# A graph-attention kernel on one core: three of four masks on GpSimd, a pair loop in fixed issue order with longer distances between its stages, and gelus in place in PSUM

## The chip, the cores and the metric

The kernel runs on one core of a Trainium2 chip. The metric is device time in microseconds (us), as the median over several executions; smaller is better. All numbers of a kernel come from the same program, once timed in rounds that alternate with the kernel before on the same chip, and once with the profiler on. A ratio given below is the mean time of one kernel's fast runs over the mean of the other's fast runs of the same rounds, so it is not quite the ratio of the two medians that I quote.

## The reference

Two layers over 3327 nodes with 64 features. Cut to what matters, with `_layernorm`, `proj`, `expmap` and the like as in any hyperbolic graph network:

```python
# layer 0, for every pair (i, j) of nodes
adj_att = sigmoid(left[:, None] + right[None, :] + b_att[0]) * adj
x_local = logmap(x[:, None, :], x[None, :, :], c)      # per pair, 64 features
support_t = einsum('ij,ijd->id', adj_att, x_local)
x = x + proj(expmap(h, support_t, c), c)
# layer 1
mask = (adj != 0)
rank = cumsum(mask, axis=1); deg = rank[:, -1:]
k = minimum(deg, 100)
pos = rank - (deg - k)
w = mask * where(pos > 0, 0.5 ** (k - pos), 0.0)
x = x + w @ (relu(layernorm(x)) @ weight) + bias
```

The kernel pads the nodes to 3328, which is 26 blocks of 128. The part that costs time is everything that has one number per pair: 3328 x 3328 of them. `logmap` is turned into a factor per pair, a product of two gelus that approximates the function of the distance, times the half-sigmoid, times `adj`; the sum over j is then a matmul. The mask and its running count for layer 1 are made in the same pass over `adj`.

## The kernel before

Columns are worked in four strips of 8, 8, 6 and 4 blocks, that is 1024, 1024, 768 and 512 columns; the last strip takes two blocks of rows at a time, so a full round is 1024 (or 768) columns wide everywhere. There are 26 + 26 + 26 + 13 = 91 rounds. `V` is VectorE, `A` ScalarE, `T` TensorE, `G` GpSimd.

```python
steps = iter(())
for b0, nb in STRIPS:
    # ... load the strip's operands; left broadcast by nb transposes and a copy
    for hi in range(NB, 0, -per):
        lo = max(hi - per, 0)
        js = range(hi - 1, lo - 1, -1)
        ad = work.tile([P, FMAX], F32, name="ad", bufs=4)
        nc.sync.dma_start(ad[...], adj_t[...])
        mask = work.tile([P, FMAX], BF16, name="mask", bufs=3)
        V.tensor_scalar(mask[:, :span], ad[:, :span], 0.0, None, op0=ALU.not_equal)
        for j in js:                                    # the running count, in PSUM
            for f0, f1 in hv:
                if before is not None:
                    T.matmul(pc[:, f0:f1], ca, before[:, f0:f1], ...)
                T.matmul(pc[:, f0:f1], cb, now[:, f0:f1], ...)
            if j % (2 if b0 == 0 else 4):               # the count is read out
                A.activation(kept, pc[:, :F], AF.Relu)
            else:
                V.tensor_scalar(kept, pc[:, :F], 0.0, None, op0=ALU.max)
        sg = work.tile([P, FMAX], F32, name="sg", bufs=3)
        for j in js:                                    # half-sigmoids
            A.activation(part(sg, j), left_b[:, :F], AF.Tanh, bias=right[:, j : j + 1], scale=0.5)
        V.scalar_tensor_tensor(sg, sg, 1.0, ad, op0=ALU.add, op1=ALU.mult)      # "sg combine"
        pq = ps.tile([P, FMAX], F32, name="pq", bufs=2)
        for j in js:                                    # products of the pair, in PSUM
            T.matmul(part(pq, j, f0, f1), ju[:KB, j, :], iuf[:, f0:f1], ...)
            T.matmul(part(pq, j, f0, f1), jz[:, j, :], izf[:, f0:f1], ...)
        s = work.tile([P, FMAX], F32, name="s", bufs=3)
        A.activation(s, pq, AF.Gelu, scale=-WG / QS)
        A.activation(s, s, AF.Gelu, scale=WH)
        V.scalar_tensor_tensor(s, s, WD, sg, op0=ALU.add, op1=ALU.mult)         # "final combine"
        for j in js:                                    # sums over j
            T.matmul(po[: D + 1, f0:f1], hw[:, j, :], part(s, j, f0, f1), ...)
            next(steps, None)                           # one step of the strip before's per-node work
    for _ in steps:
        pass
    # ... copy po out, transpose it
    steps = post(agg[:, :nb], b0, nb)
```

`post` is the per-node work of a finished strip: 17 VectorE instructions of 512 columns and, between them, 65 tiny ones of 8 columns. It is a generator that yields between groups of instructions. In this kernel the framework's scheduler decides in which order the instructions of an engine are issued; the program text only gives it priorities.

## Time and profile before

The kernel before took 461.72 us as a median of 3 runs.

In profile lines PE is TensorE and PEld its weight loads, DVE is VectorE, ACT ScalarE and POOL GpSimd; L842 is line 842 of the kernel and x91 a count. SBUF and PSUM are the two memories in which the program's tiles lie: those of the pool `ps` (`pq`, `pc`, `po`) in PSUM, all others here in SBUF.

The first lines here are from the profile page of the kernel before: busy time of each engine with its share of the span. Then groups of instructions: line, engine, operation, operands, shape, count, then busy us and mean ns of one, then idle time of the engine just before them with what ended most of it.

```profile
PE 378.4 (82%) x1484; PEld 153.4 (33%) x1484; DVE 407.1 (89%) x774; ACT 369.2 (80%) x423; POOL 13.3 (3%) x30
...
L842 DVE SCALAR_TENSOR_TENSOR sg<-sg,ad 128x1024 f32<-128x1024 f32 (+1 forms) x91 | 103.5, 1141 | 7.5 <-ACT sg L841 7.3
L852 DVE SCALAR_TENSOR_TENSOR s<-s,sg 128x1024 f32<-128x1024 f32 (+1 forms) x91 | 104.8, 1152 | 3.7 <-ACT s L851 3.6
...
L847 PE MATMUL pq<-iu,ju 71*128 71x512 f16 (+1 forms) x182 | 67.8, 374 | 11.6 <-ACT s L850 11.6
...
L824 DVE TENSOR_SCALAR mask<-ad 128x1024 bf16<-128x1024 f32 (+1 forms) x91 | 59.3, 654 | 3.4 <-PE pc L829 1.8
```

The reader should see that VectorE is the fullest engine, that masks are a seventh of its work, and that TensorE's products hardly wait (11.6 us over the whole run).

### The profile page before, as it was taken

How to read it: one execution, taken by the hardware profiler on the slowest of the kernel's cores; microseconds unless marked ns; L12 is line 12 of the kernel's file. 1: busy time of each engine (PE TensorE's matmuls, PEld its weight loads, DVE VectorE, ACT ScalarE, POOL GpSimd, SP SyncE). 2: the span in 40 equal slices, each digit the busy share in tenths (PEclk: the TensorE clock that was granted, in tenths of full speed). 3: DMA queues.
4: the chain of work that ended last, by engine and by line, in shares of the span. 5: the costliest groups of instructions: out<-in, count | busy, mean ns of one | idle time of the engine just before them, and what ended most of it. 6: DMA issues, size and time to landing. Idle time of an engine off the chain costs nothing.

```text
span 459.1 us, 4660 instructions
## 1 busy us (share of the span) xinstructions
PE 378.4 (82%) x1484; PEld 153.4 (33%) x1484; DVE 407.1 (89%) x774; ACT 369.2 (80%) x423; POOL 13.3 (3%) x30
## 2 busy tenths in 40 slices
PE   0266699999989799999997999889778897699293
PEld 0035233333323233333333444434322332244152
DVE  3895689999988999999998999999999998999821
ACT  1445989999894999999995999999599995888310
POOL 6000000000000000001000000020000000000000
PEclk9997699999999999999999999999999998899877
DMA  7103354545541444444442444344533420000003
GB/s 201 62 1 72 105 168 143 141 151 163 167 135 46 133 143 140 137 137 137 137 127 75 136 137 140 106 128 125 168 93 111 121 89 1 1 1 1 0 0 82
DMA packets 22840, 47.77 MB, mean 104 GB/s; under 512 B 8652, under 2 KB 9082, under 8 KB 22808
## 3 DMA queue, kind: packets, MB, share of 16 engines
q1 hardware_dynamic: 20522, 46.47, 34.7%
q10 hardware_dynamic: 2062, 0.87, 0.9%
q0 software_dynamic: 224, 0.07, 0.3%
q8 instruction: 13, 0.21, 0.2%
q14 instruction: 19, 0.16, 0.1%
HBM read 45.22 MB, written 0.85 MB: 100 GB/s over the span
## 4 chain that ended last, share of the span: by engine, by line

## 5 line engine op out<-in xcount | busy, mean ns | idle before, releaser
L855 PE MATMUL po<-s,hw 128*65 128x512 f32 (+1 forms) x364 | 165.3, 576 | 11.5 <-DVE s L852 11.1
L842 DVE SCALAR_TENSOR_TENSOR sg<-sg,ad 128x1024 f32<-128x1024 f32 (+1 forms) x91 | 103.5, 1141 | 7.5 <-ACT sg L841 7.3
L852 DVE SCALAR_TENSOR_TENSOR s<-s,sg 128x1024 f32<-128x1024 f32 (+1 forms) x91 | 104.8, 1152 | 3.7 <-ACT s L851 3.6
L841 ACT ACTIVATE sg<-left_b,right 128x1024 f32<-128x1024 f32 (+2 forms) x104 | 102.7, 1001 | 0.1
L851 ACT ACTIVATE s<-s 128x1024 f32<-128x1024 f32 (+1 forms) x91 | 91.4, 1006 | 0.1
L850 ACT ACTIVATE s<-pq 128x1024 f32<-128x1024 f32 (+1 forms) x91 | 87.7, 969 | 2.6 <-PE pq L848 2.6
L829 PE MATMUL pc<-mask,ca 128*128 128x512 bf16 (+1 forms) x175 | 65.7, 375 | 17.3 <-DVE behind_hi L836 7.2
L855 PEld LDWEIGHTS po<-s,hw 128*65 128x65 f32 x364 | 45.2, 138 | 98.9 <-issue 52.7
L847 PE MATMUL pq<-iu,ju 71*128 71x512 f16 (+1 forms) x182 | 67.8, 374 | 11.6 <-ACT s L850 11.6
L830 PE MATMUL pc<-mask,cb 128*128 128x512 bf16 (+1 forms) x182 | 66.7, 376 | 5.3 <-DVE mask L824 5.1
L848 PE MATMUL pq<-iz,jz 128*128 128x512 f16 (+1 forms) x182 | 66.6, 371 | 0.0
L824 DVE TENSOR_SCALAR mask<-ad 128x1024 bf16<-128x1024 f32 (+1 forms) x91 | 59.3, 654 | 3.4 <-PE pc L829 1.8
L894 PE MATMUL pw<-wt,s 128*128 128x512 bf16 (+1 forms) x182 | 41.0, 390 | 12.9 <-DVE s L782 9.2
L834 ACT ACTIVATE behind_hi<-pc 128x1024 uint8<-128x1024 f32 (+2 forms) x37 | 31.8, 860 | 24.3 <-PE pc L830 24.1
L830 PEld LDWEIGHTS <-cb 128*128 128x128 bf16 x182 | 17.9, 99 | 57.8 <-issue 46.6
L834 ACT ACTIVATE behind_lo<-pc 128x1024 uint8<-128x1024 f32 (+2 forms) x33 | 28.2, 853 | 7.1 <-PE pc L830 6.4
L894 PEld LDWEIGHTS <-s 128*128 128x128 f16 x182 | 18.7, 103 | 35.0 <-DVE s L782 9.6
L848 PEld LDWEIGHTS <-jz 128*128 128x128 f16 x182 | 18.1, 99 | 31.5 <-issue 15.3
L829 PEld LDWEIGHTS <-ca 128*128 128x128 bf16 x175 | 17.5, 100 | 30.8 <-issue 19.5
L847 PEld LDWEIGHTS <-ju 71*128 71x128 f16 x182 | 18.1, 100 | 21.4 <-issue 4.8
L836 DVE TENSOR_SCALAR behind_lo<-pc 128x1024 uint8<-128x1024 f32 (+2 forms) x19 | 19.9, 1050 | 1.1 <-PE pc L830 1.1
L771 POOL TENSOR_TENSOR x_sb<-x_sb,bias_b 128x512 f32<-128x512 f32 (+2 forms) x4 | 6.3, 1577 | 418.4 <-DVE w L769 418.4
(209 smaller groups left out, 290.0 us busy)
## 6 DMA issues: line engine op xcount, KB each, us to landing
ad<-in_adj_t SPq DMA_DIRECT2D x65, 512.0 KB, 3.7
ad<-in_adj_t SPq DMA_DIRECT2D x26, 384.0 KB, 3.3
out<-o SPq DMA_DIRECT2D x6, 128.0 KB, 2.0
x_sb<-in_x SPq DMA_DIRECT2D x1, 416.0 KB
x_sb<-in_x ACTq DMA_DIRECT2D x1, 416.0 KB, 6.9
iz<-jz ACTq DMA_DIRECT2D x2, 128.0 KB
iz<-jz SPq DMA_DIRECT2D x2, 128.0 KB, 2.4
iz<-jz SPq DMA_DIRECT2D x2, 96.0 KB
```

Source lines behind the costliest of these rows:

```text
L829: T.matmul(pc[:, f0:f1], ca, before[:, f0:f1], start=False, stop=True, skip_group_check=True)
L830: T.matmul(pc[:, f0:f1], cb, now[:, f0:f1], start=False, stop=True, skip_group_check=True)
L834: A.activation(kept, pc[:, :F], AF.Relu)
L841: A.activation(part(sg, j), left_b[:, :F], AF.Tanh, bias=right[:, j : j + 1], scale=0.5)
L842: V.scalar_tensor_tensor(sg[:, :span], sg[:, :span], 1.0, ad[:, :span], op0=ALU.add, op1=ALU.mult)
L847: T.matmul(part(pq, j, f0, f1), ju[:KB, j, :], iuf[:, f0:f1], start=True, stop=False)
L848: T.matmul(part(pq, j, f0, f1), jz[:, j, :], izf[:, f0:f1], start=False, stop=True)
L850: A.activation(s[:, :span], pq[:, :span], AF.Gelu, scale=-WG / QS)
L851: A.activation(s[:, :span], s[:, :span], AF.Gelu, scale=WH)
L852: V.scalar_tensor_tensor(s[:, :span], s[:, :span], WD, sg[:, :span], op0=ALU.add, op1=ALU.mult)
L855: T.matmul(po[: D + 1, f0:f1], hw[:, j, :], part(s, j, f0, f1), start=j == NB - 1, stop=j == 0)
L894: T.matmul(pw[n], s2[:, j].rearrange("p c d -> p (c d)"), wt[:, f0:f1].bitcast(BF16), start=j == 0, stop=j == NB - 1)
```

## The change

The intent: VectorE is full, so most masks go to GpSimd, which was idle; gelus are written back over their PSUM input, so that the final combine has only one SBUF operand; and the loop is written as a software pipeline with a fixed issue order on three engines, with loads five rounds ahead, masks four, counts three, sums two rounds behind, and no gap between strips. To make room on ScalarE, more of the count reads go to VectorE. The core of the diff, with cuts:

```diff
+AHEAD = 3
+SGB, ADB = 5, 7
+ON_ACT = ((1, 3), (1, 2), (1, 2), (1, 2))
...
+    def edges(n):
+        mask_of[n] = mask = work.tile([P, FMAX], BF16, name="mask", bufs=3)
+        args = mask[:, : span(n)], ad_of[n][:, : span(n)]
+        if n % 4 == 3:
+            V.tensor_scalar(*args, 0.0, None, op0=ALU.not_equal)
+        else:
+            G.tensor_scalar(*args, 0.0, 0.0, op0=ALU.is_equal, op1=ALU.is_equal)
...
-                if j % (2 if b0 == 0 else 4):
+        num, den = ON_ACT[k]
+        if (NB - 1 - j) % den >= den - num:
             A.activation(kept, ..., AF.Relu)
         else:
             V.tensor_scalar(kept, ..., 0.0, None, op0=ALU.max)
...
+    with tc.manual_schedule(engines={DVE, Activation, PE}):
+        products(0)
+        sigmoids(0)
+        for n in range(R):
+            m, w = n + AHEAD, span(n)
+            ...                                   # load(m + 2)
+            if turned: pa = turn(k - 1)           # transposes of the strip before
+            elif n > 1: total(n - 2)              # sums two rounds behind
+            A.activation(pq, pq, AF.Gelu, scale=-WG / QS)
+            A.activation(pq, pq, AF.Gelu, scale=WH)
+            if turned: steps = per_node(k - 1, pa)
+            V.scalar_tensor_tensor(sg, sg, 1.0, ad, op0=ALU.add, op1=ALU.mult)
+            edges(m + 1)
+            ...                                   # count(m), read(m), sigmoids(n + 1)
+            products(n + 1)
+            for _ in js(n):
+                next(steps, None)                 # a per-node step, whole, here
+            if lo == 0:
+                for _ in steps: pass
+            if ended: strip_out(k - 1)
+            V.scalar_tensor_tensor(sg, pq, WD, sg, op0=ALU.add, op1=ALU.mult)
```

Beside this the broadcast of `left` comes by DMA in strips 1 to 3 in place of transposes and a copy, a range check moves from the first change of strip to the end, and the matmul that gave each strip's count its start value is gone.

## The prediction

> **What bounds the kernel now.** I read the page's busy shares first (DVE 89%, PE 82%, ACT 80%, POOL 3%): three engines are nearly full, so an average can't name the bound. The second view is the time between two second gelus (the ScalarE line 851 in the timeline), one per round: it gives the four strips and the changes between them. The rounds run from 49 to 383 us; the gaps of 11.65, 10.86 and 11.43 us between neighbours (138.3, 242.4 and 324.6 us) are the changes of strip. The third view is the busy time of each engine in those stretches:
>
> ```profile
> core 0: us, PE busy (x) PEld busy (x) DVE busy (x) ACT busy (x) POOL busy (x), PEclk, DMA share, GB/s
> 49.00:139.00 90.00, 85.80 (x278) 30.60 (x278) 83.20 (x84) 85.06 (x89) 0.00 (x0) 0.96 0.52 154
> 150.00:242.00 92.00, 85.99 (x285) 29.89 (x283) 90.94 (x154) 91.25 (x99) 2.19 (x1) 1.00 0.48 138
> 253.00:325.00 72.00, 64.83 (x279) 29.32 (x278) 71.60 (x154) 71.15 (x98) 2.40 (x1) 1.00 0.47 134
> 336.00:383.00 47.00, 40.03 (x128) 13.23 (x126) 45.88 (x99) 45.87 (x68) 1.00 (x1) 1.00 0.35 101
> ...
> 242.00:253.00 11.00, 8.30 (x41) 3.88 (x42) 8.95 (x14) 5.78 (x9) 0.00 (x0) 1.00 0.21 67
> 325.00:336.00 11.00, 9.33 (x43) 4.00 (x42) 9.98 (x17) 5.48 (x10) 0.00 (x0) 1.00 0.35 107
> ```
>
> The reader sees: in strip 0 (first row) no vector engine is full, in strips 1 to 3 VectorE and ScalarE are both at 98 to 99%, and at a change of strip ScalarE falls to half while VectorE keeps 82 to 91%. DMA is at half.
>
> Durations overlap (the next instruction starts before the last has ended), so I take the cost of one from start to start in the timeline:
>
> ```profile
> 191.17 0.69 DVE L824 TENSOR_SCALAR mask<-ad 128x1024 bf16<-128x1024 f32 x1
> ...
> 191.77 0.69 DVE L752 TENSOR_TENSOR u<-u,w 128x512 f32<-128x512 f32 x1
> ...
> 192.37 0.38 PE L829 MATMUL pc<-mask,ca 128*128 128x512 bf16 x1
> ...
> 192.37 1.22 DVE L852 SCALAR_TENSOR_TENSOR s<-s,sg 128x1024 f32<-128x1024 f32 x1
> 192.59 0.38 PE L830 MATMUL pc<-mask,cb 128*128 128x512 bf16 x1
> ...
> 193.51 1.22 DVE L842 SCALAR_TENSOR_TENSOR sg<-sg,ad 128x1024 f32<-128x1024 f32 x1
> ```
>
> A mask costs VectorE 0.60 us (191.17 to 191.77), a combine 1.14 (192.37 to 193.51; I use 1.13, the median), a half matmul PE 0.216. Read in the same way: a count read out of PSUM 1.13 on VectorE and 0.90 on ScalarE; tanh 1.04, first gelu 0.90, second gelu 0.95 on ScalarE; the four fp32 passes of a sum 1.72 on PE (190.22 to 191.94). A PE round is 8 x 0.216 + 1.72 = 3.45 us; strip 0 ran at 90.2/26 = 3.47. So strip 0 is bound by PE, and strips 1 to 3 (rounds of 3.70, 2.86 and 3.93 us) by VectorE, with ScalarE just behind.
>
> **What the Trainium skill says.** (1) "SBUF — State Buffer", section "Who interferes with whom": GpSimd shares a port pair with VectorE; a VectorE instruction in a 2-port mode, or with two SBUF inputs against a GpSimd one that reads SBUF, excludes it for the whole instruction, and whoever comes second blocks; one SBUF input does not contend. The trace agrees. The 384-wide add on GpSimd, alone beside a PSUM read, took 1.00 us, the 256-wide one 0.73, so 512 should take 1.0 + 0.27 = 1.27; it took 2.19 behind a combine, and then a mask that takes 0.69 took 1.18 behind it:
>
> ```profile
> 215.38 1.22 DVE L852 SCALAR_TENSOR_TENSOR s<-s,sg 128x1024 f32<-128x1024 f32 x1
> 215.55 2.19 POOL L771 TENSOR_TENSOR x_sb<-x_sb,bias_b 128x512 f32<-128x512 f32 x1 [207.49 <-DVE w L769]
> 216.51 0.68 DVE L773 TENSOR_REDUCE t<-dt 128x8 f32<-128x512 f32 x1
> 217.11 1.18 DVE L824 TENSOR_SCALAR mask<-ad 128x1024 bf16<-128x1024 f32 x1
> ```
>
> (2) "GPSIMD Engine Reference", section "Engine selection": one-input work is roughly at line rate, two-input work about twice as slow; its clock is 1.2 GHz. A mask of 1024 columns is then, as an estimate from that page, 1024/1.2 = 0.85 us, and with about 0.2 of start (1.00 - 384 x 0.27/128 = 0.19 in this trace) some 1.1 us. No one-input instruction of this width is in the trace; a compare with two operations may be twice that. (3) "VectorE: DVE Perf Modes", section "Why PSUM operands drop a tier": an fp32 operand in PSUM runs at one element a cycle. The combine is already there, and a PSUM read costs the same 1.13 here as an SBUF combine, so moving its input to PSUM costs VectorE nothing. (4) "ScalarE: Activation LUTs", section "Step-by-step: what each stage is for": PSUM is the faster destination for ScalarE. Here a PSUM source gives 0.90 against 0.95 us.
>
> **The change, part by part.**
>
> Masks: of 91 rounds 3 in 4 leave VectorE: -0.75 x 0.60 = -0.45 us per 1024-wide round, -0.35 at 768 columns. Count reads move the other way: VectorE does 18 instead of 13 in strip 0 and 13 instead of 7 in the others. Strip 0: +5/26 x 1.13 = +0.22; strip 1: +6/26 x 1.13 = +0.26; strip 2: +6/26 x 0.87 = +0.20; strip 3, two reads of 512 per round: +2 x 6/26 x 0.60 = +0.28. Net on VectorE: -0.23, -0.19, -0.15, -0.17 per round. In strips 1 to 3, which it bounds: 26 x 0.19 + 26 x 0.15 + 13 x 0.17 = 11 us. Strip 0 gains nothing: PE's matmuls stay.
>
> ScalarE: second gelu out of PSUM, -0.05; fewer reads, -0.21 in strip 1: 3.40 instead of 3.66. It drops out of the race, which is needed but gains nothing itself.
>
> The combine with the gelus in place has one SBUF input, so it can't collide with a GpSimd mask; the other combine and the per-node steps can.
>
> Changes of strip: fixed order, counts three ahead, sums two behind, the broadcast of left by DMA instead of eight transposes and a copy. From 150 to 390 us VectorE's own idle time is 240 less about 232 busy, so at most 8 us come back there; I take 6. Strip 0 and its end last from 49 to 150, 101 us; PE needs 26 x 3.45 = 90 and about 4 more for the cold clock (matmuls of 0.43 until 57 us). I take 5 of the 7.
>
> Outside the rounds: range work leaves the start (about 1 us), its end moves under the decoding, left goes to memory and back: 0.
>
> GpSimd collisions: 49 masks in strips 1 to 3. A mask may start when the count two rounds later is through, which is close to the end of a VectorE round, where the contending combine starts. If one in three costs half a mask, 49 x 0.33 x 0.55 = 9 us come back.
>
> Fixed order stalls: the two-round loop final combine, products (0.86), two gelus (1.8), combine (1.13) is about 4.6 us with hops, against two rounds of 7: no stall. But an order can't fill a late wait with other work; I put -5 us of the gain on that.
>
> Sum: 461.7 - 11 - 6 - 5 + 9 + 5 = 453.7 with all the losses, 439.7 with none. I do not expect both losses in full: about 443.
>
> **The rivals.** (A) The port lock gives all back: if a mask takes 2 us and always meets a combine, each of 49 costs about 0.5, 25 us, and the time is near 461. For it: the 1.18 us mask above. Against: PSUM reads and the PSUM combine, 1.7 us of each round, are safe ground for it. (B) The fixed order is worth more than I credit: if VectorE, at 99% busy, hid waits that were only moved, the bound is PE, 84.5 full rounds x 3.45 = 292 against 341 now; with ramp and VectorE's per-node work it gives about 428. Against: VectorE's remaining work in the loop, combines 192, reads 54, per-node steps 45, masks 13, copies 4, is about 308, more than PE's, and all of the per-node part falls in strips 1 to 3. (C) GpSimd becomes the bound: it needs masks over 4/3 x 3.5 = 4.7 us; then rounds stretch and the time passes 465. I hold it unlikely, as a 512-wide two-input add takes 1.27.
>
> **Range and chances.** 443 us, from 428 (no lock, no stalls, B in part) to 457 (A almost whole). The 2% line is 452.5: faster 0.72, within 2% 0.23, slower 0.05.
>
> **What would show it.** Right: rounds of 3.45 in strip 0 and 3.5 in strip 1; gaps at the changes under 6 us; PE over 95% in strip 0; ScalarE down to 93% in strip 1; VectorE still 97% there. GpSimd masks near 1.1 us alone and 2 behind a combine, and sg combines longer than 1.22 us beside them. Wrong: GpSimd masks over 2 us; sg combines at 2 us on average (A); VectorE well under 95% in strips 1 to 3 (then stalls of the fixed order, or B); a start later than 49 us or a tail over 70.

## More of the kernel before

One measure is used throughout what follows. I take the start of the final combine of each round and add up two kinds of distance: the three gaps at which the strip changes (from the last round of one strip to the first of the next), and all others, "the rounds".

In the kernel before the loop lasts from 52.5 to 385.2 us:

| kernel before | us |
|---|---|
| ahead of the loop and after it | 126.4 |
| three changes of strip | 12.5 + 10.5 + 9.7 = 32.7 |
| the other 87 distances (rounds) | 300.1 |

## The result, and the profile after

The changed kernel took 488.3 us (487.61 to 489.47, 4 runs) against 460.49; the ratio is 1.059, 95% interval 1.051 to 1.067. It is slower by 6%. Predicted were 443 us, with 457 as the upper end of the range and a chance of 0.05 for slower.

The page of the changed kernel, with the lines that answer to those of before:

```profile
PE 378.7 (78%) x1439; PEld 157.3 (32%) x1460; DVE 423.8 (87%) x729; ACT 359.6 (74%) x397; POOL 257.3 (53%) x97
...
L859 POOL TENSOR_SCALAR mask<-ad 128x1024 bf16<-128x1024 f32 (+1 forms) x69 | 246.5, 3577 | 131.9 <-PE pc L870 59.6
...
L962 DVE SCALAR_TENSOR_TENSOR sg<-sg,ad 128x1024 f32<-128x1024 f32 (+1 forms) x91 | 109.6, 1205 | 4.8 <-DMA left_b<-left_d 4.5
L982 DVE SCALAR_TENSOR_TENSOR sg<-pq,sg 128x1024 f32<-128x1024 f32 (+1 forms) x91 | 103.8, 1141 | 3.8 <-ACT pq L959 2.9
...
L896 PE MATMUL pq<-iu,ju 71*128 71x512 f16 (+1 forms) x182 | 69.6, 383 | 23.6 <-DVE sg L982 23.0
...
L871 PE MATMUL pc<-mask,cb 128*128 128x512 bf16 (+1 forms) x174 | 64.8, 382 | 14.8 <-POOL mask L859 12.6
```

Three things stand out. A mask of 1024 columns takes GpSimd 3.6 us (masks that follow each other at once start 3.59 us apart), not the 1.1 that I had estimated; yet TensorE waited for a GpSimd mask only 12.6 us in all, and that is a wait ahead of the loop, so GpSimd is not the bound. VectorE is busy for longer although 69 masks left it. And the products now wait 23 us for the final combine of two rounds earlier, twice what they waited before, for another engine.

Busy time in the four strips and after them (columns as in the prediction: stretch, its length, then each engine's busy time with its count, granted clock, DMA share, GB/s):

```profile
51.00:142.00 91.00, 87.58 (x291) 32.67 (x296) 88.84 (x83) 86.32 (x87) 71.84 (x20) 0.98 0.50 149
142.00:252.00 110.00, 94.76 (x304) 34.13 (x308) 103.27 (x154) 89.63 (x95) 70.63 (x20) 0.95 0.41 118
252.00:348.00 96.00, 78.12 (x326) 35.45 (x329) 91.22 (x160) 79.09 (x106) 64.92 (x22) 0.96 0.45 128
348.00:413.00 65.00, 49.62 (x147) 17.91 (x148) 57.14 (x122) 47.95 (x67) 25.81 (x8) 0.89 0.17 49
```

In strips 1 to 3 VectorE is at 94, 95 and 88%, ScalarE at 81, 82 and 74%: the other engines fall away and VectorE stays the bound. The loop by the measure of above:

| us | before | changed |
|---|---|---|
| ahead of the loop and after it | 126.4 | 125.5 |
| three changes of strip | 32.7 | 2.5 + 2.4 + 3.7 = 8.5 |
| rounds | 300.1 | 351.9 |

So the gaps between strips closed, 24 us less, as meant; and the rounds, which should have become shorter, became 52 us longer. By strip, from the final combine of one strip's first round to that of the next strip's: 99.4 to 92.0, 102.6 to 111.8, 83.0 to 93.0, and in strip 3 (its twelve distances) 47.7 to 63.7. The loss is in strips 1 to 3, where per-node work runs beside the rounds: without the changes of strip their rounds take 17, 16 and 16 us more. Those of strip 0, which has no per-node work, take 2.5 us more (87.0 to 89.5), so strip 0 won by its closed gap alone.

What fills VectorE there is seen in its timeline. First the kernel before (start us, duration, engine, line, operation, shape):

```profile
185.44 0.22 DVE L739 SCALAR_TENSOR_TENSOR t<-y,c_c,xy 128x8 f32<-128x8 f32 x1
185.58 0.16 DVE L741 TENSOR_TENSOR t<-t,xy 128x8 f32<-128x8 f32 x1
185.66 1.22 DVE L852 SCALAR_TENSOR_TENSOR s<-s,sg 128x1024 f32<-128x1024 f32 x1
186.79 0.17 DVE L742 TENSOR_SCALAR t<-t 128x8 f32<-128x8 f32 x1
186.87 0.69 DVE L824 TENSOR_SCALAR mask<-ad 128x1024 bf16<-128x1024 f32 x1
187.47 0.20 DVE L743 RECIPROCAL t<-t 128x8 f32<-128x8 f32 x1
187.58 1.17 DVE L842 SCALAR_TENSOR_TENSOR sg<-sg,ad 128x1024 f32<-128x1024 f32 x1
```

Then the same place of the changed kernel:

```profile
178.16 1.22 DVE L962 SCALAR_TENSOR_TENSOR sg<-sg,ad 128x1024 f32<-128x1024 f32 x1
179.29 0.17 DVE L504 TENSOR_SCALAR rs_t<-t 128x8 int32<-128x8 int32 x1
179.49 0.17 DVE L505 TENSOR_SCALAR rn<-rs_t 128x8 int32<-128x8 int32 x1
...
181.10 0.17 DVE L509 TENSOR_TENSOR rs_t<-rs_t,rs_g 128x8 f32<-128x8 f32 x1
181.30 0.17 DVE L510 SCALAR_TENSOR_TENSOR rn<-rs_t,rn 128x8 f32<-128x8 f32 x1
181.50 0.17 DVE L736 TENSOR_TENSOR t<-t,rn 128x8 f32<-128x8 f32 x1
181.59 0.19 DVE L737 RECIPROCAL t<-balm 128x8 f32<-128x8 f32 x1
181.81 1.09 DVE L738 SCALAR_TENSOR_TENSOR t<-t,sqc,t 128x8 f32<-128x8 f32 x1
182.83 1.21 DVE L982 SCALAR_TENSOR_TENSOR sg<-pq,sg 128x1024 f32<-128x1024 f32 x1
```

A tiny instruction before a large, independent one costs 0.08 to 0.11 us from start to start (185.58 to 185.66, 186.79 to 186.87, 187.47 to 187.58). One that waits for the tiny one before it costs 0.20 (179.29 to 179.49, 181.10 to 181.30). The scheduler had strewn the chain between large instructions; the fixed order issues a step in one piece, here fifteen instructions and 3.5 us, in front of the final combine at 182.83. In the loop and just behind it, tiny instructions take 43.3 us of VectorE from start to start (205 of them) against 23.4 (201) before. Not all of this is the order: some of them are held up by GpSimd masks, as the account behind e7 shows. Counted over the loop, a tiny instruction follows the one that it needs 130 times (median 0.201 us from start to start) against 26 before, and an independent large one follows a tiny one 25 times against 124 (medians 0.083 and 0.077). TensorE stands behind the same place; these are its products (in brackets: idle time before, and what ended it):

```profile
184.10 0.38 PE L896 MATMUL pq<-iu,ju 71*128 71x512 f16 x1 [2.18 <-DVE sg L982]
...
191.80 0.39 PE L896 MATMUL pq<-iu,ju 71*128 71x512 f16 x1 [2.40 <-DVE sg L982]
```

Also in that stretch: the GpSimd mask that starts at 181.85 meets the tiny instruction of 181.81, which takes 1.09 instead of 0.22 us.

```profile
181.85 3.62 POOL L859 TENSOR_SCALAR mask<-ad 128x1024 bf16<-128x1024 f32 x1 [3.19 <-PE pc L870]
```

The mask runs to 185.47, and while it does, a final combine (one SBUF operand) and a sg combine (two) start at 182.83 and 183.97 and take 1.21 us, the usual time. Over the whole run, 23 sg combines of 1024 columns started more than 1 us after a GpSimd mask that still ran and took 1.215 us on average; 11 that started within its first microsecond took 1.60, at most 2.07. So a mask holds such an instruction up for some 0.85 us at its start and not for its whole length.

For strips 1 to 3 (142 to 415 us against 143 to 392) the account of VectorE, from start to start, is: tiny instructions with their gaps +19, reads +14, idle time +9, sg combines +3, masks -21, the other large work +1: about +25.

### The profile page after: what moved, and what is told of

Read it like the earlier page. It is cut to its first block, busy times and chain, and to the rows that moved or that the text cites. A ratio compares the mean times of both kernels' runs of the same rounds, so it can differ in the third digit from the quotient of the medians.

```text
span 485.9 us, 4824 instructions
## 1 busy us (share of the span) xinstructions
PE 378.7 (78%) x1439; PEld 157.3 (32%) x1460; DVE 423.8 (87%) x729; ACT 359.6 (74%) x397; POOL 257.3 (53%) x97
## 4 chain that ended last, share of the span: by engine, by line
## 5 line engine op out<-in xcount | busy, mean ns | idle before, releaser
L859 POOL TENSOR_SCALAR mask<-ad 128x1024 bf16<-128x1024 f32 (+1 forms) x69 | 246.5, 3577 | 131.9 <-PE pc L870 59.6
L906 PE MATMUL po<-sg,hw 128*65 128x512 f32 (+1 forms) x364 | 168.6, 588 | 3.4 <-DVE sg L982 3.2
L962 DVE SCALAR_TENSOR_TENSOR sg<-sg,ad 128x1024 f32<-128x1024 f32 (+1 forms) x91 | 109.6, 1205 | 4.8 <-DMA left_b<-left_d 4.5
L982 DVE SCALAR_TENSOR_TENSOR sg<-pq,sg 128x1024 f32<-128x1024 f32 (+1 forms) x91 | 103.8, 1141 | 3.8 <-ACT pq L959 2.9
L958 ACT ACTIVATE pq<-pq 128x1024 f32<-128x1024 f32 (+1 forms) x91 | 86.6, 952 | 21.0 <-PE pq L897 20.1
L959 ACT ACTIVATE pq<-pq 128x1024 f32<-128x1024 f32 (+1 forms) x91 | 86.2, 947 | 2.9
L870 PE MATMUL pc<-mask,ca 128*128 128x512 bf16 (+1 forms) x166 | 63.0, 380 | 29.2 <-DVE behind_hi L882 15.3
L906 PEld LDWEIGHTS po<-sg,hw 128*65 128x65 f32 x364 | 51.6, 144 | 77.8 <-issue 60.1
L871 PE MATMUL pc<-mask,cb 128*128 128x512 bf16 (+1 forms) x174 | 64.8, 382 | 14.8 <-POOL mask L859 12.6
L882 DVE TENSOR_SCALAR behind_hi<-pc 128x1024 uint8<-128x1024 f32 (+2 forms) x30 | 30.9, 1030 | 4.6 <-PE pc L871 3.7
L882 DVE TENSOR_SCALAR behind_lo<-pc 128x1024 uint8<-128x1024 f32 (+2 forms) x27 | 28.0, 1038 | 2.3 <-PE pc L871 2.2
L1010 PEld LDWEIGHTS <-s 128*128 128x128 f16 x182 | 18.8, 104 | 33.1 <-DVE s L791 9.6
L880 ACT ACTIVATE behind_lo<-pc 128x1024 uint8<-128x1024 f32 (+2 forms) x25 | 21.0, 838 | 11.0 <-PE pc L871 10.8
L897 PEld LDWEIGHTS <-jz 128*128 128x128 f16 x182 | 18.5, 101 | 30.6 <-issue 15.8
```

The lines of the kernel that those rows point to most:

```text
L859: G.tensor_scalar(*args, 0.0, 0.0, op0=ALU.is_equal, op1=ALU.is_equal)
L870: T.matmul(S.pc[:, f0:f1], ca, S.before[:, f0:f1], start=False, stop=True, skip_group_check=True)
L871: T.matmul(S.pc[:, f0:f1], cb, now[:, f0:f1], start=S.first, stop=True, skip_group_check=True)
L897: T.matmul(part(n, pq, j, f0, f1), jz[:, j, :], S.iz[:, f0:f1], start=False, stop=True)
L906: T.matmul(S.po[: D + 1, f0:f1], hw[:, j, :], part(n, sg_of[n], j, f0, f1), start=j == NB - 1, stop=j == 0)
L958: A.activation(pq, pq, AF.Gelu, scale=-WG / QS)
```

## The experiments

All were timed in three rounds beside the kernel before, e16 in five. The medians of the kernel before in those rounds lie between 460.1 and 461.5 us. "Fixed order" is the changed kernel's, "scheduler's order" is the changed kernel with the same program text but the order left to the scheduler.

**e1: the per-node work finer, in the fixed order.** Theory A: a step issued in one piece in front of the final combine is the loss. Rival B: the GpSimd masks are. Rival C: the fixed order of the large instructions.

```diff
-            for _ in js(n):
-                next(steps, None)
+    # post_fine: yields after each instruction; feed(steps, 2) issues two, at four places of the round:
+    # after the sg combine, after the first read (strip 3 only), before and after the final combine
```

> The changed kernel with one thing different: the per-node work is issued one instruction at a time between the large VectorE instructions of a round, not a whole step (up to 15 dependent small ones) in one place. Order, engines and amount of work are otherwise the same. Theory A (the loss is the chains of small dependent instructions, 0.2 us each in a row against 0.08 when something stands between, and the waits behind them; 43 us of small instructions in the loop against 23): some 20 to 28 us come back, 460 to 468 us, and the small instructions cost under 28 us in the loop. Theory B (the loss is the port that GpSimd and VectorE share): within 5 us of the changed kernel's 488. Theory C (any fixed order loses): over 480.

Measured: 484.25 us, ratio 1.053 (1.048 to 1.058), correct. It fits what B and C expected, and A as I had tried it missed. The timeline shows why this edit did not do what it was to do: two tiny instructions beside each other still depend on each other and still cost 0.20 or more, and a mask's 0.85 us still falls on tiny ones:

```profile
183.59 0.22 DVE L886 TENSOR_SCALAR xy<-xy,m2c 128x8 f32<-128x8 f32 x1
183.85 0.17 DVE L888 TENSOR_SCALAR xy<-xy 128x8 f32<-128x8 f32 x1
183.93 1.22 DVE L1118 SCALAR_TENSOR_TENSOR sg<-sg,ad 128x1024 f32<-128x1024 f32 x1
185.06 1.00 DVE L890 SCALAR_TENSOR_TENSOR t<-y,c_c,xy 128x8 f32<-128x8 f32 x1
185.98 0.21 DVE L892 SCALAR_TENSOR_TENSOR t<-y,c_c,x 128x8 f32<-128x8 f32 x1
```

So this run, whose edit left the tiny instructions as dear as they were (43.6 us for 197 in the loop, 42.7 for 203 in the changed kernel), can't decide between the theories; it shows that this hand-made interleaving in fixed places isn't enough. One thing it did change: the products' wait for the final combine fell from 23.0 to 9.5 us, yet only 4 us of time came back, while TensorE's counts waited longer for VectorE's reads (26.7 us, 19.3 in the changed kernel). So that one wait is not by itself what the fixed order loses.

**e2: the scheduler's order.**

```diff
-    with tc.manual_schedule(engines={DVE, Activation, PE}):
+    with ExitStack():
```

> The changed kernel without the fixed order: the scheduler orders the pair loop as it did before the change; masks on GpSimd, gelus in PSUM and all else stay. Theory A: the small instructions are spread again, 455 to 470 us. Theory B: 480 to 490, as every mask still meets VectorE. Theory C: well under 470, with no gaps of over 2 us of PE waiting for the final combine.

Measured: 456.34 us, ratio 0.992 (0.988 to 0.996), correct. One line gives back 32 of the 488.3 us: the fixed order is the loss, and the sum of all other parts is a small gain (4 us). Rounds 306.6, changes of strip 10.1. VectorE there:

```profile
181.43 1.21 DVE L982 SCALAR_TENSOR_TENSOR sg<-pq,sg 128x1024 f32<-128x1024 f32 x1
182.57 0.15 DVE L510 SCALAR_TENSOR_TENSOR rn<-rs_t,rn 128x8 f32<-128x8 f32 x1
182.64 1.21 DVE L962 SCALAR_TENSOR_TENSOR sg<-sg,ad 128x1024 f32<-128x1024 f32 x1
183.78 1.01 DVE L508 TENSOR_TENSOR rs_t<-rn 128x8 f32<-128x8 f32 x1
184.71 1.21 DVE L982 SCALAR_TENSOR_TENSOR sg<-pq,sg 128x1024 f32<-128x1024 f32 x1
```

One link of the chain sits between two large instructions and costs 0.07; a mask's start makes some of them take 1.01 (25 of 346 tiny instructions took over 0.6 us here, 12 in the changed kernel).

**e3: how much the masks on GpSimd disturb.** GpSimd writes zeros in place of comparing; the result is wrong (relative error 0.88).

```diff
-            G.tensor_scalar(*args, 0.0, 0.0, op0=ALU.is_equal, op1=ALU.is_equal)
+            G.memset(args[0], 0.0)
```

> Wrong result on purpose: each GpSimd mask is a memset of the same tile, which reads no SBUF and should be far shorter than 3.6 us; all else as in the changed kernel. It takes away the contention for the read port and any lateness of masks. Theory A: only some 10 us come back (masks on VectorE 1.1 to 0.7 us, combines 1.28 to 1.22, a few small ones of 1.0 us), 475 to 482. Theory B: 20 us or more, under 468.

Measured: 477.14 us, ratio 1.036 (1.031 to 1.040). The 69 instructions took 0.95 us at 1024 columns and read no SBUF; sg combines of 1024 columns were back at 1217 ns (1280 in the changed kernel). So the compare in place of a memset costs 11 us, not the 30 that are lost. This is not the whole price of the masks: the memset holds VectorE up too. Its own 22 masks took 0.78 us each from start to start beside the memsets, 0.57 in e4, where no mask runs on GpSimd.

**e4: all masks on VectorE, in the fixed order.**

```diff
-        if n % 4 == 3:
+        if True:
```

> The changed kernel with all masks on VectorE (the GpSimd part undone), fixed order and the rest kept. VectorE gets 68 masks of 0.6 us back (38 us) and loses the contention (about 10). Theory A: slower, 505 to 520 us, as VectorE is the bound. Theory B: no slower than the changed kernel, at or under 488.

Measured: 495.08 us, ratio 1.077 (1.072 to 1.082), correct. Above the one expectation's limit and below the other's range, so both missed: the masks on GpSimd are worth 7 us in the fixed order.

**e5: the count reads divided as before, in the fixed order.**

```diff
-        num, den = ON_ACT[k]
-        if (NB - 1 - j) % den >= den - num:
+        if j % (2 if k == 0 else 4):
```

> The changed kernel, fixed order kept, with the count reads split as before the change (70 on ScalarE, 34 on VectorE, not 47 and 57). Theory D (VectorE is the bound, and every us put on it counts): VectorE loses 23 reads, about 15 us of the loop, and ScalarE, busy only 80% in strip 1, has room for them: 470 to 477 us. Theory C (in the fixed order the time is in waits of one engine for another, not in VectorE's load): within 5 us of 488.

Measured: 474.25 us, ratio 1.028 (1.022 to 1.035), correct, as expected. The reads that moved to VectorE cost 14 us.

**e6: both edits, of e2 and of e5.**

```diff
-    with tc.manual_schedule(engines={DVE, Activation, PE}):
+    with ExitStack():
-        if (NB - 1 - j) % den >= den - num:
+        if j % (2 if k == 0 else 4):
```

> Scheduler's order (as in the run without the fixed order, 456 us) and the count reads split as before the change. Theory D: VectorE is still the bound there, so 443 to 450 us. Theory C: ScalarE takes over as the bound or the reads were hidden, 453 to 460.

Measured: 445.79 us, ratio 0.968 (0.962 to 0.974), correct. This version beats both kernels, 15 us ahead of the kernel before. Between e5 and e6 only the order differs: 28.5 us. Strips 1 to 3 of it:

```profile
143.00:242.00 99.00, 91.42 (x320) 34.41 (x319) 95.06 (x149) 95.64 (x106) 72.04 (x21) 1.00 0.44 128
242.00:324.00 82.00, 73.46 (x325) 34.37 (x323) 79.87 (x148) 77.24 (x108) 63.72 (x21) 1.00 0.47 133
324.00:370.00 46.00, 40.41 (x134) 14.30 (x133) 44.14 (x92) 42.72 (x64) 23.30 (x7) 1.00 0.20 58
```

VectorE is at 96 to 97% and ScalarE at 93 to 97%: nearly balanced, unlike the changed kernel's 94 to 81.

**e7: the scheduler's order with all masks on VectorE**, the edits of e2 and e4.

```diff
-    with tc.manual_schedule(engines={DVE, Activation, PE}):
+    with ExitStack():
-        if n % 4 == 3:
+        if True:
```

> Scheduler's order, all masks on VectorE: the GpSimd part undone on its own. It measures what the masks on GpSimd are worth when no fixed order is in the way. If the move pays (38 us of masks off VectorE against about 10 us of blocking): 475 to 485 us against 456. If the lock gives all back: 452 to 460.

Measured: 469.39 us, ratio 1.018 (1.012 to 1.025), correct. In between, against e2's 456.34: the masks on GpSimd are worth 13 us here.

Runs e4 and e7 have the same instructions, no GpSimd masks, and differ in the order alone: 25.7 us. Their traces, beside those of the changed kernel and e2, say where the time of VectorE goes (whole run, from start to start of the next, idle time over 0.15 us left out):

| VectorE, us | 346 tiny | 91 sg combines | one mask of its own (mean) |
|---|---|---|---|
| e4, fixed order, no GpSimd masks | 55.2 | 96.7 | 0.57 |
| e7, scheduler's order, no GpSimd masks | 39.4 | 96.7 | 0.57 |
| changed, fixed order | 64.1 | 104.8 | 0.97 |
| e2, scheduler's order | 56.8 | 98.4 | 0.62 |

Two things follow. Without GpSimd masks the order costs 15.8 us on the tiny instructions, most of its 25.7 us: in the loop of e4 133 of them follow the one that they need (median 0.200 us), in e7 6, and 127 stand before an independent large one (0.076). And the 69 masks take 39 us off VectorE but make its other instructions last longer, by the sum of their durations 24 us in the changed kernel against e4 (tiny 9.2, its own 22 masks 8.9, sg combines 5.5) and 22 in e2 against e7 (tiny 18.8); by the same account it is 24 us in e6 against e16. The order alone, e4 against e7, changes these durations by 1 us. It fits that e4 and e7, whose expectations counted about 10, both fell in between.

**e8: the fixed order without the per-node work of strips 0 to 2**, wrong (0.416).

```diff
-                steps = per_node(k - 1, pa)
+                steps = iter(())
```

> Wrong result on purpose: the changed kernel, fixed order, without the per-node work of strips 0 to 2 (the 3 x 26 us of it that VectorE showed in the loop, with its waits). If the per-node work put in one place is what the fixed order loses by, the strips then run at PE's pace (3.45, 3.45, 2.6, 3.45 us a round, loop about 300 us) and the whole at 425 to 435 us, 55 to 60 less. If the order of the large work is what loses, only its own work goes (3 x 18 us) or less: 440 to 455.

Measured: 430.33 us, ratio 0.935 (0.929 to 0.940), as the first expectation has it (the edit also sets the missing result to zero). Without it the fixed order runs at TensorE's pace in strips 0 and 1:

```profile
53.00:142.00 89.00, 88.70 (x303) 33.70 (x302) 85.32 (x81) 85.43 (x87) 70.34 (x19) 0.99 0.53 156
142.00:231.00 89.00, 87.27 (x307) 33.88 (x306) 77.15 (x71) 84.44 (x88) 63.44 (x19) 0.98 0.48 141
```

PE is busy for 88.70 and 87.27 of 89 us, and by the final combines strips 0 and 1 take 89.9 and 92.5 us. So the loop as the change's author drew it works; what it can't carry is the work that was hung into it.

**e9: the same with only the tiny instructions gone**; the large ones of the per-node work stay, eight memsets stand for the rest, wrong (0.393).

```diff
-        return post(agg[:, :nb], b0, nb)
+        return (post_big if k < len(STRIPS) - 1 else post)(agg[:, :nb], b0, nb)
+        # post_big: for q in (sa, t0, t1, k, y2, u2, xy, rn): V.memset(q, 0.0); then the large ones only
```

> Wrong result on purpose: the changed kernel, fixed order, where the per-node steps of strips 0 to 2 keep their 18 large VectorE instructions each but lose the 60 small ones (8 memsets stand for them). Of the 58 us that the whole per-node work costs in the fixed order, the small ones' share. Theory A (the dependent chains of small instructions are the larger part): 445 to 460 us. If the large ones and the waits they bring are the larger part: 465 to 478.

Measured: 452.11 us, ratio 0.981 (0.974 to 0.987). Of the 58 us that the per-node work costs in the fixed order (488.3 - 430.3), the tiny instructions are 36 and the large ones 22. (The expectation's 18 large and 60 tiny ones per strip are rough; they are 17 and 65.)

**e10: as e8, but in the scheduler's order.**

```diff
-    with tc.manual_schedule(engines={DVE, Activation, PE}):
+    with ExitStack():
-                steps = per_node(k - 1, pa)
+                steps = iter(())
```

> Wrong result on purpose: the scheduler's order without the per-node work of strips 0 to 2. Against its own 456 us it gives the price of that work when it is spread. If the fixed order loses by how it places the per-node work and by nothing else, this run is no faster than the fixed order without it (430 us): 425 to 435, the price about 26 to 30 against 58. If the fixed order is bad for the large work too, this run is clearly faster, under 422.

Measured: 420.23 us, ratio 0.912 (0.906 to 0.918), wrong in the same way. The per-node work costs 36 us in the scheduler's order (456.3 - 420.2) against 58 in the fixed one; and the fixed order costs 10 us on the large work alone (430.3 - 420.2). So the 32 us are 22 from where the per-node work stands and 10 from the rest. The second expectation holds. By the final combines, 6.6 us of the rest lie in strip 3 (46.5 us in e8, 39.9 here), where a round takes two blocks of rows, and about 5 in strips 1 and 2.

**e11: the kernel before with nothing but the masks moved.** This is the part that I had predicted as a gain of itself.

```diff
-            V.tensor_scalar(mask[:, :span], ad[:, :span], 0.0, None, op0=ALU.not_equal)
+            if rnd % 4 == 3:
+                V.tensor_scalar(mask[:, :span], ad[:, :span], 0.0, None, op0=ALU.not_equal)
+            else:
+                nc.gpsimd.tensor_scalar(mask[:, :span], ad[:, :span], 0.0, 0.0, op0=ALU.is_equal, op1=ALU.is_equal)
+            rnd += 1
```

> The kernel before with one part of the change alone: three of four masks on GpSimd, gelus still into SBUF, so that both combines have two SBUF inputs. The scheduler's order with all of the change but the fixed order gained 13 us from the GpSimd masks. If the move of the gelus to PSUM is what makes the masks pay: 455 to 470 us here. If the lock hardly matters (about 0.16 us per mask, as the memset run says): 445 to 452, the same gain of 10 to 15 us.

Measured: 482.94 us, ratio 1.051 (1.043 to 1.060), correct: slower than either expectation. Both combines were longer, and the sums waited:

```profile
L857 DVE SCALAR_TENSOR_TENSOR s<-s,sg 128x1024 f32<-128x1024 f32 x65 | 87.0, 1342 | 10.0 <-ACT s L856 10.0
L847 DVE SCALAR_TENSOR_TENSOR sg<-sg,ad 128x1024 f32<-128x1024 f32 x65 | 85.0, 1315 | 10.4 <-ACT sg L846 10.3
```

Before, the same two took 1225 and 1217 ns. That is 65 x (0.117 + 0.098) = 14 us. The tiny instructions were held up still more: 62.4 us from start to start in the whole run, 41.4 before. By durations all groups together last 36 us longer, against 39 us of masks that left VectorE, and 68 tiny instructions follow the one that they need (26 before). So the move relieved VectorE of nothing here: from start to start it is busy 4 us longer, and some 17 of the 21 us that the profiled run lost are waits. The masks waited 60 us for the DMA of `adj`, and the sums 28.6 us for the final combine. What loads and sums have to do with it was tried in the next four runs.

**e12: the same, with the gelus in place in PSUM** and the final combine written over `sg` (five buffers), so that it has one SBUF operand, as in the change.

```diff
-            s = work.tile([P, FMAX], F32, name="s", bufs=3)
-            A.activation(s, pq, AF.Gelu, scale=-WG / QS)
-            A.activation(s, s, AF.Gelu, scale=WH)
-            V.scalar_tensor_tensor(s, s, WD, sg, ...)
+            A.activation(pq, pq, AF.Gelu, scale=-WG / QS)
+            A.activation(pq, pq, AF.Gelu, scale=WH)
+            V.scalar_tensor_tensor(sg, pq, WD, sg, ...)
```

> The kernel before with three of four masks on GpSimd, as in the run before this one (482.9 us), and the gelus now in place in PSUM: the final combine reads PSUM and writes over the half-sigmoids (five buffers), the gelu buffers are gone; the loads of adj keep their four buffers, the order is the scheduler's. If masks alone failed because GpSimd and the final combine fought for SBUF (it took 1.32 us there, 1.22 before): final combines back at 1.22 us and the time at 445 to 455. If they failed because a mask of 4 us on GpSimd comes too late with four buffers of adj and three of the mask: 470 to 485, with the masks still waiting for the DMA. Between 455 and 470: both.

Measured: 506.77 us, ratio 1.099 (1.093 to 1.106), correct. A plain miss, outside all three expectations. The final combine was indeed undisturbed, but the sums and the products stood in line:

```profile
L860 PE MATMUL po<-sg,hw 128*65 128x512 f32 (+1 forms) x364 | 174.0, 606 | 40.4 <-DVE sg L856 39.0
L847 DVE SCALAR_TENSOR_TENSOR sg<-sg,ad 128x1024 f32<-128x1024 f32 (+1 forms) x91 | 107.6, 1186 | 33.4 <-ACT sg L846 33.3
L846 ACT ACTIVATE sg<-left_b,right 128x1024 f32<-128x1024 f32 (+2 forms) x104 | 101.1, 982 | 29.5 <-PE po L860 29.3
L856 DVE SCALAR_TENSOR_TENSOR sg<-pq,sg 128x1024 f32<-128x1024 f32 (+1 forms) x91 | 103.8, 1141 | 23.2 <-ACT pq L855 23.1
```

VectorE waits 33 and 23 us for ScalarE, which waits 29 us for TensorE's sums, which wait 39 us for VectorE. This is a ring: the tanh of a later round needs a free `sg` buffer, and since the final combine now writes over `sg`, a buffer comes free only after its sum; and a sum issued right behind that combine keeps TensorE waiting ahead of the products.

**e13: e11 with six buffers of `adj` in place of four.**

```diff
-            ad = work.tile([P, FMAX], F32, name="ad", bufs=4)
+            ad = work.tile([P, FMAX], F32, name="ad", bufs=6)
```

> The kernel before with three of four masks on GpSimd (482.9 us with four buffers of adj), now with six buffers of adj. If late loads are the cause of its loss (masks waited 60 us for the DMA there): 455 to 468 and the masks' wait for the DMA under 20 us. If the lock on both combines or the masks' 4 us in line with the counts is the cause: 478 to 486.

Measured: 485.81 us, ratio 1.052 (1.045 to 1.059), correct. Late loads are not the cause: the masks' wait for the DMA fell from 60 to 21 us (20 of it a single wait), that for TensorE's counts (to free a mask buffer; two lines) rose from 58 to 79, and the time did not move.

**e14: e12 with the sums two rounds behind.**

```diff
-            for j in js:
-                for f0, f1 in hv:
-                    T.matmul(po[...], hw[:, j, :], part(s, j, f0, f1), ...)
+            sums.append((js, lo, s))
+            if len(sums) > 2:
+                total(*sums.pop(0))
```

> Masks on GpSimd and gelus in place in PSUM in the kernel before (506.8 us), now with the sums issued two rounds behind, as in the change; four buffers of adj. If sums that follow at once stood in front of the products on TensorE (39 us of waits for the final combine there): 470 to 485, with that wait under 15 us. If only the loads or masks are late: 500 to 510.

Measured: 468.87 us, ratio 1.016 (1.009 to 1.023), correct: 38 us better than e12. The sums' wait for the final combine fell from 39 to 2 us, as the lines show, and a wait of the products for it took part of its place (with the gelus in place a PSUM buffer is held until the final combine has read it):

```profile
L818 PE MATMUL po<-sg,hw 128*65 128x512 f32 (+1 forms) x364 | 167.0, 580 | 1.9 <-DVE sg L863 1.9
...
L859 PE MATMUL pq<-iu,ju 71*128 71x512 f16 (+1 forms) x182 | 68.6, 377 | 29.8 <-DVE sg L863 29.0
```

**e15: e14 with seven buffers of `adj`.**

```diff
-            ad = work.tile([P, FMAX], F32, name="ad", bufs=4)
+            ad = work.tile([P, FMAX], F32, name="ad", bufs=7)
```

> As the run before, with seven buffers of adj in place of four. If late loads and early sums are all that was missing: 444 to 455, as the version with the scheduler's order (445.8). If the counts issued three rounds ahead are needed too, because a mask of 4 us stands in line with its own round's counts: 465 or more.

Measured: 470.20 us, ratio 1.020 (1.013 to 1.027), correct; the buffers give nothing. Against e6 (445.79) it lacks the counts ahead and the closed gaps between strips. By the measure of the final combines its rounds are nearly as long as e6's, 309.2 against 307.8, and its three changes of strip take 35.1 us against 8.5: that is about the whole difference.

**e16: e6 with all masks on VectorE**, five rounds. The missing corner: all of the new loop but not the masks.

```diff
-        if n % 4 == 3:
+        if True:
```

> The version with the scheduler's order and the reads on ScalarE (445.8 us), now with all masks on VectorE. If the gains add up, the masks are worth 13 us as they were with the reads on VectorE: 457 to 461, which is the kernel before, so the new order of rounds would be worth nothing by itself. If closing the gaps between strips (24 us less there) is a gain of its own: 440 to 452. If the new order needs the room that the masks leave on VectorE: 463 or more.

Measured: 452.77 us, ratio 0.981 (0.977 to 0.986), correct. A hair above the second expectation's range, far from the other two. The new distances and closed gaps gain 9 us without GpSimd; the masks on GpSimd add 7.

Together, by the final combines of the profiled runs (us):

| kernel | median | three changes of strip | rounds |
|---|---|---|---|
| before | 460.5 | 32.7 | 300.1 |
| changed | 488.3 | 8.5 | 351.9 |
| e2, scheduler's order | 456.3 | 10.1 | 306.6 |
| e6, and reads as before | 445.8 | 8.5 | 307.8 |
| e16, and all masks on VectorE | 452.8 | 9.7 | 304.7 |
| e11, before + masks on GpSimd | 482.9 | 33.7 | 323.9 |
| e12, + gelus in PSUM | 506.8 | 32.4 | 353.3 |
| e14, + sums two behind | 468.9 | 33.7 | 311.8 |

Medians and these sums do not move together to the last microsecond: what stands ahead of the loop and after it lies between 122 us (e11) and 137 us (e2, e16), as per-node work finishes earlier or later.

## Why the prediction was wrong

The prediction had the right sign for almost every term and put the largest one at a sixth of its size. I walk from the kernel before to the changed one by the runs; the steps add up by construction, and another path divides them a little differently.

| term | predicted | measured | runs |
|---|---|---|---|
| changes of strip, longer distances, gelus in PSUM | -11 | -9 | before to e16 |
| masks to GpSimd, the lock included | -26.7 + 9 = -18 | -7 (-13 with the reads on VectorE) | e16 to e6 (e7 to e2) |
| count reads to VectorE | +15.6 | +11 (+14 in the fixed order) | e6 to e2 (changed to e5) |
| fixed order | +5 | +32 (+28 with the reads as before, +26 without GpSimd masks) | e2 to changed (e6 to e5, e7 to e4) |

(The prediction gives masks and reads as one net gain of 11; the split is its own arithmetic: masks 26 x 0.45 + 26 x 0.35 + 13 x 0.45 = 26.7, reads 26 x 0.26 + 26 x 0.20 + 13 x 0.28 = 15.6.)

**The step that failed** is "Fixed order stalls: the two-round loop final combine, products (0.86), two gelus (1.8), combine (1.13) is about 4.6 us with hops, against two rounds of 7: no stall." The loop was timed with the bare durations of its own instructions. In strips 1 to 3 VectorE issues per-node steps between them, and I never asked where in the fixed order these stand. They stand in front of the final combine, whole: 3.5 us for a reciprocal square root and what hangs on it, at 0.20 us for each dependent link where the scheduler's strewing paid 0.08. The products of the round after next wait behind that combine, and TensorE and ScalarE with them. e8 shows that it is the per-node work: with it gone the loop does what I computed in strips 0 and 1, PE at 98 to 100%. e10 sizes it: 22 of the 32 us. The other 10 us are lost on the large work alone, 6.6 of them in strip 3; that is more than my 5, and what in the fixed order loses them I have not shown. That the dependent links cost VectorE's own time is shown by e4 and e7, without any GpSimd mask: 15.8 of 25.7 us. With the masks the order also decides what they hit: from e2 to the changed kernel the tiny instructions take 7.3 us more, the sg combines 6.4 and VectorE's own masks 7.8; the rest is waiting. How much the wait of the products adds was not separated; e1, which more than halved it, got 4 us back. e1 also shows that the cure is not simply to cut the steps finer.

**The choice of 443.** The terms summed to 453.7 with all losses, and I took 443 because I "do not expect both losses in full". Both came in full, and one six times over. The uncertainty of the fixed order was cut off at 5 us on the side of loss, so that the range had no room for this result, and no rival named it; B even had the fixed order as a gain. ("VectorE well under 95% in strips 1 to 3 (then stalls of the fixed order, or B)" did stand among the signs; it came at 94, 95 and 88%.) The range's upper end, 457, was also below rival A's own 461, and A's terms, 439.7 + 25, give 465.

**The mask on GpSimd.** Estimated 1.1 us, measured 3.6. "GpSimd masks over 2 us" stood among the signs that would make the prediction wrong, but it was not what did: rival C's line was 4.7 us, and GpSimd stayed at 53%. For the lock the prediction had 9 us in strips 1 to 3. That e3 gave 11 is luck: a memset holds VectorE up too, and the 9 rested on a wrong picture, half of a 1.1 us mask met by one in three. From e4 to the changed kernel VectorE's other instructions became 24 us longer in the whole run, about 14 of them in strips 1 to 3, and over a third of it is on its own masks, which the prediction's list of what a GpSimd mask can hit leaves out. Rival A had 25 there and all of the gain lost, so it falls too, but by less than e3 alone makes it seem: what the moved masks brought, 7 to 13 us, is less than the 18 predicted.

**Masks as a gain by themselves.** The prediction took them off VectorE's sum per round. Its own first table has ScalarE as full as VectorE in strip 1 (91.25 and 90.94 of 92 us), so "ScalarE just behind" was a loose reading, and relief for VectorE alone need not show; that the masks gain 7 us where ScalarE keeps its reads and 13 where it does not would fit this, but it was not tested. e11 shows that in the old loop the same edit loses 23 us. In e11 to e15 the buffers of `adj` changed nothing, sums two behind repaired 38 us where gelus were in PSUM, and what was left of the difference to e6 sits in the changes of strip. In e11 longer instructions took nearly all that VectorE was to gain (36 of 39 us); what makes the waits that are the rest of its loss was not separated.

**What held.** Strip 0 bound by TensorE (87.58 of 91 us busy); gaps at the changes of strip under 6 us (2.5, 2.4, 3.7); the final combine with its PSUM operand undisturbed (1217 ns, before 1225) and sg combines longer than 1.22 (1.28); the reads' cost. "Rounds of 3.5 us in strip 1" became 4.3 (111.8 / 26), and ScalarE there fell to 81%, below the 93 that I had named; its largest wait was for products (20.1 us), and theirs for the final combine (23.0). The 24 us less at the changes of strip are no pure gain: VectorE was at 81 to 91% in those gaps before (8.95 of 11 us is 81%, not 82), and its work there has to go elsewhere. In e16, which has 23 us less at the changes, the rounds take 4.6 us more (300.1 to 304.7) and the stretches ahead of the loop and after it 10.5 us more; 8 us are left in the profiled runs and 9 in the medians, near the 11 predicted.

## What to carry to other kernels

If an engine that sets the pace also carries chains of tiny dependent instructions, a fixed issue order must place each link between large independent instructions; time the loop with that work in it, not without. Moving work to an idle engine is worth what it takes away less what it then holds up on the engine that was to be relieved: here 39 us less 22 to 24, and less 36 in the old loop. And its longer latency has to be bought with distance (here the sums two rounds behind and no drained pipeline between strips), so test such a move together with the distances and again alone. And after a compound change has failed, undo its parts one by one: the version with the scheduler's order and the reads left on ScalarE, 445.8 us, was two small edits away from one of 488.

## What the Trainium skill lacked or had wrong

- "GPSIMD Engine Reference", section "Engine selection", calls one-input work roughly line-rate. Here a compare with two operations from fp32 to bf16 took GpSimd 3.62 us at 1024 columns when little disturbed it (3.59 from start to start; mean 3.84, and 2.93 at 768 columns), where VectorE took 0.69 for its compare with one. Only a memset of the same tile came near such a rate, with 0.95 us.
- "SBUF — State Buffer", section "Who interferes with whom", calls the shared port pair an exclusive lock and says that a VectorE instruction with two SBUF inputs contends with a GpSimd one that reads SBUF. Here the lock did not last as long as the GpSimd instruction: a mask of 3.62 us held such an instruction up by some 0.85 us at the mask's start (1.09 instead of 0.22, and 1.01 instead of 0.15 in e2; sg combines up to 2.07), while 23 sg combines that started later inside a mask took 1.215 on average. With 69 masks VectorE's instructions came to last 22 to 24 us longer in all (e2, the changed kernel, e6). That an operand in PSUM keeps clear of it agrees: final combines took 1217 ns beside masks in the changed kernel, 1215 without in e4.
- "VectorE: DVE Perf Modes", section "The TRN2 errata — SBUF-src ops pay a fixed extra latency per instruction", says that many small tiles pay a fixed latency each. The runs add what it lacks, the part that the next instruction has in it: an instruction of 8 columns costs 0.20 us from start to start if the next one needs its result, and 0.07 to 0.11 if an independent large one follows. For the same 346 tiny instructions this was 55.2 against 39.4 us (e4 and e7).
